# A state-space scan and windowed attention on one core: when a row is scaled, and how the inverse key sums reach the partitions that need them

## The chip, the cores and the metric

The kernel runs on one core of a Trainium2 chip. A core has TensorE (matrix products, "PE" in the profile, with its weight loads as "PEld"), VectorE ("DVE"), ScalarE ("ACT"), GpSimd ("POOL") and SyncE ("SP"), which here only issues transfers. Each engine works through its own list of instructions in order and waits at the head of the list until the inputs of the next instruction are there. The metric is device time in microseconds of one execution; lower is better.

## What is computed

The input `x` has 32 sequences of 256 tokens with 256 channels each. Two networks follow each other, and `x` is added to the result at the end. All is in 32-bit floating point. The first is a gated state-space layer; its core is a scan over the tokens:

```python
xr, gate = jnp.split(x @ W_in.T, 2, axis=-1)          # 512 channels each
xc = silu(causal_conv4(xr + t_emb[:, None, :]))
xn = layernorm(xc) * ln_g + ln_b
Bm, Cm, dt = jnp.split(xn @ W_xproj.T, 3, axis=-1)     # 16 states each
Ad = 1.0 + tanh(dt @ W_dt.T + b_dt) * 0.01 * -tanh(A_log)
Bd = Bm * minimum(norm(xn), 1.0)
def step(h, inputs):                                   # 256 steps, one after the other
    ad, bd, xt, ct = inputs
    h = jnp.clip(h * ad[:, :, None] + bd[:, :, None] * xt[:, None, :], -10.0, 10.0)
    return (h, jnp.einsum('bd,bdh->bh', ct, h))
y = (ys + D * xn) * silu(gate) @ W_out.T
```

The second is two layers of attention in windows of 128 tokens (each window sees itself and the one before), with 8 heads of 64, followed by a gated feed-forward part:

```python
q, k, v = heads(shift_token(x) @ wqkv)
q, k = rotary(l2norm(q) * qs, l2norm(k) * ksc)
attn = softmax(where(mask, -max, 8.0 * q @ k.T))
x = x + (attn @ v) @ wo
a, g = split(layernorm(shift_token(x)) @ w1 + b1)
x = x + (a * gelu(g)) @ w2 + b2
```

## The kernel before

**Groups and sequences.** The 32 sequences are worked in 4 groups of 8 (`GB`). The scan of a group holds the 8 sequences times 16 states on the 128 partitions and the 512 channels in the free dimension; it takes 256 steps, in 8 chunks of 32 (`CH`). Attention and feed-forward then take one sequence and one layer at a time: 4 groups x 2 layers x 8 sequences = 64 passes, called "sequences" below. While attention works on group g, the scan of group g + 1 runs beside it. The first scan group therefore has no attention beside it, and the last attention group no scan.

**A step of the scan.** The normalised tokens of a chunk are stored to device memory (`xnd`). For each token, `load_rows` (line 634) loads its 8 rows back, each repeated over 16 partitions, into a tile `xrep` of [128, 512] from the pool `xp`, which has 7 buffers. `scale_row` (line 654) multiplies it in place on ScalarE by a factor per partition, `beta`, which is computed once per chunk (lines 579 to 606). `step` (line 662) adds it to the state and clips, on VectorE, and frees the buffer. `read_out` (line 672) forms four steps' outputs on TensorE (`y`). In the first group, half of the rows come from a product on TensorE instead (`spread_rows`, line 639). The text asks for the load of token t at slot t - 6, for the scaling at t - 1 and for the step at t (lines 838 to 854).

**Attention of one sequence.** `scores` (line 1103) forms key-by-query products and their exponentials `pT` on ScalarE. `sums` (line 1131) adds them over the keys with a product by ones, so that the sum of head h stands on 16 partitions, and takes the reciprocal `rinv` on VectorE (line 1145): [128, 256], where the 8 heads lie at every 16th partition. `values` (line 1148) forms the unnormalised output `oT`, [128, 4, 256]: four pairs of heads, 64 partitions per head. `divide` (line 1166) must therefore bring the inverse sum of each head to the 64 partitions of its output. It does so with a product on TensorE by a table of ones and zeros, `head_rows` (filled in `head_table`, line 354), into PSUM tiles `rb`, and VectorE multiplies. `finish` calls `project_out` (line 958), whose product is `ps_wo`. `FeedForward` follows: `normalise`, `apply` and `spread` (layer norm, with a power on GpSimd), `widen` (product `pa`, then gelu to `ag` on ScalarE), `product`, and `narrow` (product `po_f`). The exponential and the gelu need different function tables on ScalarE, so a table load stands between them where they alternate.

**What sets the order.** The program text first lists the work by stages: 8 stages (`ST`) per sequence, and each part of sequence n gets a stage (lines 1332 to 1371); between stages, a proportional number of scan slots is put in. The compiler's scheduler then orders each engine's list from that text. It keeps dependences, and takes next what is ready first by its own model of durations, with the order of the text as priority. An instruction given to `keep_in_program_order` is issued after every instruction of its engine that stands before it in the text; for all others the scheduler may move them ahead. Transfers are issued by SP in the order that results, each after the events that it waits for; a load of `xrep` waits until the step that used the buffer before is done. All PSUM tiles share one pool of 8 banks.

Of the kernel before, what the change touches and what calls it, by code (L numbers as in the profile page):

```python
# [10 lines left out]
FP = mybir.dt.float32  # L11
# [8 lines left out]
P = 128  # L20
S = 256
# [15 lines left out]
HEADS = 8  # L37
DH = 64
# [35 lines left out]
def kernel(  # L74
# [29 lines left out]
    nc = tc.nc  # L104
# [4 lines left out]
    const = ctx.enter_context(tc.tile_pool(name="const", bufs=1))  # L109
# [35 lines left out]
    ident = const.tile([P, P], FP, tag="ident", name="ident")  # L145
# [17 lines left out]
    for j in range(NJ):  # L163
# [18 lines left out]
        out=mask_t[:, 0:W], in_=mask_t[:, 0:W], compare_op=ALU.is_ge, fill=MASKED_LOW,  # L182
# [3 lines left out]
        out=mask_t[:, W : 2 * W], in_=mask_t[:, W : 2 * W], compare_op=ALU.is_ge,  # L186
        fill=MASKED_LOW, base=0, pattern=[[-1, W]], channel_multiplier=1,
    )


    head_cols = const.tile([P, 2, 32], FP, tag="head_cols", name="head_cols")
    nc.gpsimd.memset(head_cols, 0.0)
    head_rows = const.tile([P, HEADS, DH], FP, tag="head_rows", name="head_rows")
    for r in range(2):
        nc.gpsimd.memset(head_cols[:, r, r * 16 : (r + 1) * 16], 1.0)
    rc_sb = const.tile([P, L, NW, 2, DH], FP, tag="rc_sb", name="rc_sb")
# [19 lines left out]
    for i in range(2):  # L216
        t = const.tile([P, NI * (P + GB)], FP, tag=f"ly{i}", name=f"ly{i}")
# [3 lines left out]
    def program(ctx, exact):  # L221
# [14 lines left out]
        def constants(at):  # L236
# [117 lines left out]
            def head_table(h):  # L354
                row = 32 * (h // 2) + 16 * (h % 2)
                tc.keep_in_program_order(
                    nc.gpsimd.tensor_copy(
                        head_rows[:, h, :], ident[:, row : row + 1].broadcast_to([P, DH])
                    )
                )  # L360

            at(-43, load_w)
            at(-34, fold_1)
            at(-32, fold_2)
# [20 lines left out]
        def group_scan(g):  # L385
# [14 lines left out]
            def at(s, what, *args):  # L400
                agendas[-1].setdefault(s, []).append(partial(what, *args))
# [252 lines left out]
            def scale_row(c, t):  # L654
                if by_tensor(t):
                    ck[c]["rep", t] = xp.tile([P, DI], FP, tag="xrep", name="xrep")
                bx = ck[c]["rep", t]
                nc.scalar.activation(  # L658
                    bx, ck[c].pop(("bx", t), bx), AF.Copy, scale=ck[c]["beta"][:, t : t + 1]
                )  # L660

            def step(c, t):
                bx = ck[c].pop(("rep", t))
# [174 lines left out]
            for c in range(NCH):  # L838
                s0 = c * CH
                at(s0 - 43, load_x, c)  # L840
                for ch in range(NC_):
                    at(s0 - 40 + 2 * ch, project, c, ch)
                for ch, s in enumerate((13, 16, 17, 18)):
                    at(s0 + s, project, c, NC_ + ch)
                at(s0 - 27, raw_sums, c)
                for j in range(NJ):
                    at(s0 - 26 + 4 * j, norm_turn, c, j)
                at(s0 - 8, figures_out, c)
                for t in range(CH):
# [227 lines left out]
        class Attention:  # L1077
# [70 lines left out]
            def values(self, b):  # L1148
# [14 lines left out]
                    nc.scalar.copy(oT[:, i0 : i0 + 2], ov)  # L1163
                self.o[b] = oT

            def divide(self, b):
                for i0 in range(0, HEADS // 2, 2):
                    rb = ps_w.tile([P, 2, S], FP, tag="w", name="rb")
                    for i in range(2):
                        h = 2 * (i0 + i)  # L1170
                        nc.tensor.matmul(
                            rb[:, i],
                            head_rows[:, h : h + 2].rearrange("p r d -> p (r d)"),
                            self.rinv,
                            start=True,
                            stop=True,
                        )
# [151 lines left out]
        def stage(n, i, what, *args):  # L1329
            stages.setdefault(ST * n + i, []).append(partial(what, *args))  # L1330

        def attend(n, at, b, nxt):

            stage(n, 0, at.turn, b, 1)
            stage(n, 3, at.scores, b, 0, 0, 2)
            stage(n, 2, at.scores, b, 1, 0, HEADS // 2)
            stage(n, 5, at.scores, b, 0, 2, 2)
            stage(n, 7, at.sums, b)
            stage(n, 7, at.values, b)
            stage(n + 1, 2, at.divide, b)  # L1340
            stage(n + 1, 5, at.finish, b)
            if nxt is not None:
                for w in range(NW):
                    for i, a in ((0, 2), (1, 0), (1, 1)):
                        stage(n, 3 * w + i, nxt[0].project, nxt[1], w, a)
                stage(n, 6, nxt[0].turn, nxt[1], 0)

        def feed(n, g, l, b):
            ff = FeedForward(g, l, b)
            for w in range(NW):  # L1350
                stage(n + 1, 7 + w, ff.normalise, w)
                stage(n + 2, 0 + w, ff.apply, w)
                stage(n + 2, 1 + w, ff.spread, w)
            for m in range(NM):
                stage(n + 2, 3 + m, ff.widen, m)
                stage(n + 2, 4 + m, ff.product, m)
            for d in range(KM):
                stage(n + 3, 2 + d, ff.narrow, d)

        def fetch(n, g, l, b):  # L1360

            if b == GB - 1 and (g, l) != (NG - 1, L - 1):
                nl = (l + 1) % L
                for i, a in ((5, 2), (6, 0), (6, 1)):
                    stage(n - 1, i, load_weights, nl, "qkv", a)
                stage(n + 1, 7, load_weights, nl, "wo")
                for m in range(NM):
                    stage(n + 2, 5 + m, load_weights, nl, "w1", m)
                stage(n + 3, 5, load_weights, nl, "w2")
            if l == L - 1 and g < NG - 1:  # L1370
                stage(n + 6, 2, load_res, g + 1, b)

# [159 lines left out]
```

## Time and profile before

The median of three runs is 3999.52 us (3998.8 to 4003.98). The profiled execution took 3989.48 us, and its span, from the first to the last instruction, is 3987.7 us at a mean granted TensorE clock of 0.983.

| Work | Line | Engine | Count | One |
|---|---|---|---|---|
| product `rb` (recorded as two passes per instruction) | 1171 | PE | 512 | 379 ns |
| multiplication `oT` by `rb`, 128x512 | 1179 | DVE | 128 | 676 ns |
| reciprocal `rinv`, 128x256 | 1145 | DVE | 64 | 1748 ns |
| scaling of a loaded row | 658 | ACT | 896 | 722 ns |
| step of the scan | 665 | DVE | 1024 | 807 ns |
| table loads before exponentials and gelus | 1127, 1255 | ACT | 185 and 186 | 1283 ns |
| loads of rows, 256 KB each | 637 | SP | 896 | 515 ns to issue |

Times are those of the profile's groups and tiles (medians where it gives them). A group's busy time counts overlapping instructions once. "Idle before" a group is the time that its engine stood still just before, and the name after the arrow is what ended it. The stretches, the waits and the timeline are views of the same recording; a sequence of the attention is repeated at a fixed distance in time in the last stretch, so that one can be read for all.

The lines that follow are the first groups of the costliest, with their idle time and releaser at the end:

```profile
L658 ACT ACTIVATE xrep<-xrep,beta 128x512 f32<-128x512 f32 x896 | 631.1, 722 | 692.2 <-DMA xrep<-xnd 532.4
L665 DVE CUSTOM_DVE_ANT_0 h<-h,xrep,lim 128x512 f32<-128x512 f32 x1024 | 918.6, 897 | 52.7 <-PE y L677 12.5
L912 PE MATMUL ps_qkv<-qkv,res 128*128 128x512 f32 x1536 | 718.0, 604 | 34.6 <-ACT qT L956 21.7
```

### The profile page before, as it was taken

The numbers are of one execution on the slowest core, as the hardware profiler recorded it, in microseconds if no ns is written. First come the engines' busy times: TensorE is split into PE (matmuls) and PEld (weight loads), VectorE is DVE, ScalarE is ACT, GpSimd is POOL, SyncE is SP. The second block draws the span as 40 slices with busy tenths as digits, with TensorE's granted clock in tenths as the row PEclk, the third lists the DMA queues.
The fourth block names the chain that finished last, engine by engine and source line by source line (L and its number), as shares of the span: only waits on it lengthen the run. The fifth ranks groups of instructions, "written<-read, shape, count | busy, mean of one in ns | idle before, by whom it ended". The sixth has DMA issues, their size and how long they took to land.

```text
span 3987.7 us, 57891 instructions
## 1 busy us (share of the span) xinstructions
PE 3769.4 (95%) x20540; PEld 2359.2 (59%) x20540; DVE 2638.7 (66%) x5241; ACT 2321.3 (58%) x3893; POOL 1739.2 (44%) x1784
## 2 busy tenths in 40 slices
PE   7899889999999999999999999999999999999999
PEld 3333345666656666666666666566666666666666
DVE  6888887777766766767676677676677544444443
ACT  3555556666666566566666656556666555555553
POOL 4443364444444444544445444344444343433431
PEclk8999899999999999999999999999999999999999
DMA  5444533333433434233343434323333111000000
GB/s 152 116 119 118 159 111 110 89 107 103 106 98 97 124 109 128 84 93 94 91 112 94 118 106 116 101 83 101 94 101 103 36 36 44 1 17 20 18 14 23
DMA packets 360414, 353.51 MB, mean 89 GB/s; under 512 B 173795, under 2 KB 220212, under 8 KB 359988
## 3 DMA queue, kind: packets, MB, share of 16 engines
q1 hardware_dynamic: 275666, 337.71, 29.4%
q10 hardware_dynamic: 84450, 12.01, 1.9%
q8 instruction: 165, 2.70, 0.3%
q14 instruction: 133, 1.09, 0.1%
HBM read 314.49 MB, written 33.55 MB: 87 GB/s over the span
## 4 chain that ended last, share of the span: by engine, by line
PE 44%; DVE 16%; ACT 13%; DMA 11%; POOL 9%; issue 5%; ACTq 1%; SPq 0%; DVEq 0%; POOLq 0%
DMA xrep<-xnd 10%; PE ps_qkv L912 9%; PE pa L1247 8%; PE po_f L1275 5%; DVE h L665 5%; PE y L677 3%; ACT xrep L658 3%; PE ps_wo L962 3%; PE sc L1118 3%; PE ov L1156 2%; POOL rn L944 2%; ACT L1255 2%; DVE acc L454 2%; PE ps_in L407 2%; ACT L1127 2%
## 5 line engine op out<-in xcount | busy, mean ns | idle before, releaser
L658 ACT ACTIVATE xrep<-xrep,beta 128x512 f32<-128x512 f32 x896 | 631.1, 722 | 692.2 <-DMA xrep<-xnd 532.4
L665 DVE CUSTOM_DVE_ANT_0 h<-h,xrep,lim 128x512 f32<-128x512 f32 x1024 | 918.6, 897 | 52.7 <-PE y L677 12.5
L912 PE MATMUL ps_qkv<-qkv,res 128*128 128x512 f32 x1536 | 718.0, 604 | 34.6 <-ACT qT L956 21.7
L1247 PE MATMUL pa<-hT,w 128*128 128x256 f32 (+1 forms) x3072 | 693.0, 388 | 28.0 <-ACT pT L1127 26.8
L936 POOL TENSOR_TENSOR rot<-rot,swp 128x512 f32<-128x512 f32 x256 | 344.1, 1344 | 766.3 <-DVE swp L933 621.5
L1247 PEld LDWEIGHTS pa<-hT,w 128*128 128x128 f32 (+1 forms) x3072 | 502.4, 179 | 192.1 <-issue 63.3
L1263 DVE SCALAR_TENSOR_TENSOR ag<-pa,b_sb,ag 128x256 f32<-128x256 f32 (+1 forms) x448 | 213.1, 476 | 594.6 <-ACT ag L1255 593.2
L912 PEld LDWEIGHTS ps_qkv<-qkv,res 128*128 128x128 f32 x1536 | 279.2, 192 | 314.6 <-issue 247.4
L944 POOL TENSOR_TENSOR rn<-ss,neg_half 128x8 f32<-128x8 f32 x256 | 444.2, 1735 | 11.5 <-DVE ss L942 1.6
L1275 PE MATMUL po_f<-ag,w 128*128 128x256 f32 (+1 forms) x1536 | 385.4, 392 | 17.9 <-DVE res L1286 9.3
L677 PE MATMUL y<-h,ly 128*32 128x512 f32 x2048 | 369.1, 620 | 20.1 <-DVE h L665 19.5
L1275 PEld LDWEIGHTS po_f<-ag,w 128*128 128x128 f32 (+1 forms) x1536 | 273.9, 189 | 124.3 <-issue 44.4
L407 PE MATMUL ps_in<-xg,w_in_sb 128*128 128x256 f32 x1024 | 285.9, 410 | 18.0 <-DMA xg<-in_xT_dram 10.4
L945 POOL TENSOR_TENSOR rot<-rot,rn 128x512 f32<-128x512 f32 x256 | 287.7, 1124 | 20.0
L1206 POOL TENSOR_TENSOR rstd<-ve,neg_half 128x1 f32<-128x1 f32 x128 | 77.0, 602 | 486.6 <-DVE ve L1204 486.6
L407 PEld LDWEIGHTS ps_in<-xg,w_in_sb 128*128 128x128 f32 x1024 | 190.8, 199 | 145.7 <-issue 62.0
L928 DVE TENSOR_TENSOR rot<-ps_qkv,rc_sb 128x512 f32<-128x512 f32 x256 | 175.6, 686 | 139.0 <-ACT sq L925 137.8
L1127 ACT ACTIVATE pT<-sc 128x512 f32<-128x512 f32 x384 | 208.3, 594 | 94.9 <-PE sc L1118 93.3
L454 DVE SCALAR_TENSOR_TENSOR acc<-xr,wc_sb,acc 128x256 f32<-128x256 f32 x384 | 203.4, 532 | 89.2 <-POOL acc L443 88.1
L1127 ACT ACT_TABLE_LOAD x185 | 237.4, 1283 | 24.5 <-PE sc L1118 21.5
L1255 ACT ACTIVATE ag<-pa,b_sb 128x256 f32<-128x256 f32 x320 | 151.7, 474 | 156.8 <-PE pa L1247 152.4
L1255 ACT ACT_TABLE_LOAD x186 | 238.6, 1283 | 3.3
(149 smaller groups left out, 5765.7 us busy)
## 6 DMA issues: line engine op xcount, KB each, us to landing
xrep<-xnd SPq DMA_DIRECT2D x896, 256.0 KB
xnd<-xn SPq DMA_DIRECT2D x64, 256.0 KB
qkv<-in_wqkv_dram SPq DMA_DIRECT2D x24, 512.0 KB
xd<-xnd SPq DMA_DIRECT2D x192, 64.0 KB
w<-in_w_dram SPq DMA_DIRECT2D x80, 128.0 KB
xg<-in_xT_dram SPq DMA_DIRECT2D x64, 128.0 KB
ys<-yo ACTq DMA_DIRECT2D x64, 128.0 KB
res<-ys SPq DMA_DIRECT2D x32, 256.0 KB
```

Of the source, the lines that this page charges most:

```text
L407: nc.tensor.matmul(ps, w_in_sb[:, k, ch * P : (ch + 1) * P], ck[c]["xg"][:, k], start=(k == 0), stop=(k == KM - 1),)
L658: nc.scalar.activation(bx, ck[c].pop(("bx", t), bx), AF.Copy, scale=ck[c]["beta"][:, t : t + 1])
L665: nc.vector._custom_dve(TENSOR_ADD_SAT, out=h_new, in0=state["h"], in1=bx, s0=ck[c]["lim"][:, 0, t : t + 1], s1=ck[c]["lim"][:, 1, t : t + 1],
L677: nc.tensor.matmul(ck[c]["y", hb][32 * q : 32 * q + 32, :], ly[hb % 2][:, 32 * t : 32 * t + 32], ck[c].pop(("h", hb * TB + t)), start=(i = ...
L912: nc.tensor.matmul(ps, res[b][:, k, t0 : t0 + W], wt["qkv", a][:, k], start=(k == 0), stop=(k == KM - 1),)
L936: nc.gpsimd.tensor_add(rot, rot, swp)
L944: nc.gpsimd.tensor_tensor(rn, ss, neg_half, ALU.pow)
L945: nc.gpsimd.tensor_mul(rot, rot, bc(rn, 2, DH))
L1127: nc.scalar.activation(p, banks[r], AF.Exp)
L1247: nc.tensor.matmul(pg if x else pa, wt["w1", m][:, k, x], self.h[:, k], start=(k == 0), stop=(k == KM - 1),)
L1255: nc.scalar.activation(ag[0:n], pg, AF.Gelu, bias=b1g)
L1275: nc.tensor.matmul(self.po[:, d], wt["w2", 0][r0 : r0 + n, m, d * P : (d + 1) * P], self.ag[m][r0 : r0 + n], start=(m == 0), stop=(m == le ...
```

## The change

There are three edits, and what follows from them.

1. *Scaling.* From the second group on, each scaling is given to `keep_in_program_order`, and all scalings are asked for one slot earlier (t - 2 instead of t - 1).
2. *Inverse sums.* The product by `head_rows` and the table itself go. `put_inverse` stores the 8 rows of `rinv` (8 KB) to a tile `inv` in device memory; `load_inverse` reads it back twice, for the even and for the odd heads, each row repeated over 64 partitions, into `rb`, [128, 4, 256], now in SBUF (one buffer). `divide` becomes one multiplication. The tile takes space in SBUF, and `xp` has 6 buffers instead of 7.
3. *Stages.* Store, load, multiplication and output product get the stages 0, 2, 4 and 6 of the next sequence's time (the multiplication was at 2, the output product at 5), and the feed-forward and the weight loads that belong to it come one stage later.

```diff
-    head_rows = const.tile([P, HEADS, DH], FP, tag="head_rows", name="head_rows")
...
-        xp = ctx.enter_context(tc.tile_pool(name="xp", bufs=7, reuse_waits="tile"))
+        xp = ctx.enter_context(tc.tile_pool(name="xp", bufs=6, reuse_waits="tile"))
...
-            for h in range(HEADS):
-                at(100 + 2 * h, head_table, h)
...
-                nc.scalar.activation(
+                scaled = nc.scalar.activation(
                     bx, ck[c].pop(("bx", t), bx), AF.Copy, scale=ck[c]["beta"][:, t : t + 1]
                 )
+                if not alone:
+
+                    tc.keep_in_program_order(scaled)
...
-                    at(s0 + t - 1, scale_row, c, t)
+                    at(s0 + t - 2, scale_row, c, t)
...
+            def put_inverse(self):
+                self.inv = dp.tile([HEADS, S], FP, tag="inv", name="inv")
+                nc.sync.dma_start(out=self.inv, in_=self.rinv[0 : P : P // HEADS])
+
+            def load_inverse(self):
+
+                rb = ap_.tile([P, HEADS // 2, S], FP, tag="rb", name="rb", bufs=1)
+                inv = self.inv.rearrange("(i r) t -> r i t", r=2)
+                for r in range(2):
+                    nc.sync.dma_start(out=rb[r * DH : (r + 1) * DH], in_=bc(inv[r], 0, DH))
+                self.rb = rb
+
             def divide(self, b):
-                for i0 in range(0, HEADS // 2, 2):
-                    rb = ps_w.tile([P, 2, S], FP, tag="w", name="rb")
-                    for i in range(2):
-                        h = 2 * (i0 + i)
-                        nc.tensor.matmul(
-                            rb[:, i],
-                            head_rows[:, h : h + 2].rearrange("p r d -> p (r d)"),
-                            self.rinv,
-                            start=True,
-                            stop=True,
-                        )
-                    o = self.o[b][:, i0 : i0 + 2]
-                    nc.vector.tensor_mul(o, o, rb)
+                nc.vector.tensor_mul(self.o[b], self.o[b], self.rb)
...
-            stage(n + 1, 2, at.divide, b)
-            stage(n + 1, 5, at.finish, b)
+            stage(n + 1, 0, at.put_inverse)
+            stage(n + 1, 2, at.load_inverse)
+            stage(n + 1, 4, at.divide, b)
+            stage(n + 1, 6, at.finish, b)
...
-                stage(n + 1, 7 + w, ff.normalise, w)
-                stage(n + 2, 0 + w, ff.apply, w)
-                stage(n + 2, 1 + w, ff.spread, w)
+                stage(n + 1, 8 + w, ff.normalise, w)
+                stage(n + 2, 1 + w, ff.apply, w)
+                stage(n + 2, 2 + w, ff.spread, w)
             for m in range(NM):
-                stage(n + 2, 3 + m, ff.widen, m)
-                stage(n + 2, 4 + m, ff.product, m)
+                stage(n + 2, 4 + m, ff.widen, m)
+                stage(n + 2, 5 + m, ff.product, m)
             for d in range(KM):
-                stage(n + 3, 2 + d, ff.narrow, d)
+                stage(n + 3, 3 + d, ff.narrow, d)
```

Each engine's list is ordered anew by the scheduler for the changed text, so instructions that no edit names can stand elsewhere than before.

More of the change, by code (lines that the diff above doesn't have):

```diff
@@ L352, in tables @@
                 )
[L354 to L358, printed above, removed]
-                    )
-                )
             at(-43, load_w)
@@ L1164, in values @@
                 self.o[b] = oT
-            def divide(self, b):
-                for i0 in range(0, HEADS // 2, 2):
-                    rb = ps_w.tile([P, 2, S], FP, tag="w", name="rb")
-                    for i in range(2):
-                        h = 2 * (i0 + i)
-                        nc.tensor.matmul(
-                            rb[:, i],
-                            head_rows[:, h : h + 2].rearrange("p r d -> p (r d)"),
-                            self.rinv,
-                            start=True,
-                            stop=True,
-                        )
-                    o = self.o[b][:, i0 : i0 + 2]
-                    nc.vector.tensor_mul(o, o, rb)
+            def put_inverse(self):
[7 more added lines that the diff above has]
+                self.rb = rb
+            def divide(self, b):
+                nc.vector.tensor_mul(self.o[b], self.o[b], self.rb)
             def finish(self, b):
@@ L1365, in fetch @@
                     stage(n - 1, i, load_weights, nl, "qkv", a)
-                stage(n + 1, 7, load_weights, nl, "wo")
+                stage(n + 2, 0, load_weights, nl, "wo")
                 for m in range(NM):
-                    stage(n + 2, 5 + m, load_weights, nl, "w1", m)
-                stage(n + 3, 5, load_weights, nl, "w2")
+                    stage(n + 2, 6 + m, load_weights, nl, "w1", m)
+                stage(n + 3, 6, load_weights, nl, "w2")
             if l == L - 1 and g < NG - 1:
```

## The prediction

> **What bounds the kernel now.** I read the page's engine shares first, then the busy time by stretch, then the waits, and last single stretches of the timeline.
>
> ```profile
> PE 3769.4 (95%) x20540; PEld 2359.2 (59%) x20540; DVE 2638.7 (66%) x5241; ACT 2321.3 (58%) x3893; POOL 1739.2 (44%) x1784
> ```
>
> TensorE is busy in 95% of the span, VectorE (DVE) in 66%. The stretches say where the missing 5% lies. Columns: stretch, its length, busy microseconds (and instructions) of PE, weight load, DVE, ACT and POOL, granted clock, DMA share, GB/s.
>
> ```profile
> 0.00:487.00 487.00, 415.00 (x1552) 170.10 (x1552) 410.62 (x769) 264.08 (x489) 198.57 (x289) 0.93 0.47 129
> 487.00:600.00 113.00, 102.41 (x516) 53.40 (x516) 90.14 (x162) 59.87 (x108) 70.10 (x62) 0.91 0.44 127
> 600.00:3100.00 2500.00, 2373.68 (x13434) 1529.42 (x13435) 1756.72 (x3486) 1559.24 (x2618) 1137.75 (x1148) 0.99 0.37 103
> 3130.00:3900.00 770.00, 770.00 (x4412) 527.82 (x4406) 332.59 (x732) 393.73 (x606) 314.39 (x267) 1.00 0.08 22
> 3900.00:3988.00 88.00, 78.36 (x442) 59.66 (x438) 27.00 (x59) 27.91 (x49) 7.80 (x9) 0.98 0.06 20
> ```
>
> There are three regimes: the first scan group alone (to 487), scan and attention side by side (to 3100), and attention alone (to the end). In the last, TensorE never stops: 770.00 of 770. In the middle it is idle for 2500 - 2373.7 = 126.3 us, and for 10.6 more in 487 to 600. So work taken off TensorE is gained nearly in full there, and 137 us of stalls are the second thing to win.
>
> The product that the change removes, by the same stretches (PE, weight load, DVE only), and one run of it at the end:
>
> ```profile
> 600.00:3100.00 2500.00, 81.51 (x344) 61.92 (x344) 55.38 (x86) 0.99 0.37 103
> 3130.00:3900.00 770.00, 34.06 (x144) 25.96 (x144) 24.75 (x36) 1.00 0.08 22
> ```
>
> ```profile
> 3937.37 1.89 PE L1171 MATMUL rb<-rinv,head_rows 128*128 128x256 f32 x8
> 3939.10 2.95 PE L1275 MATMUL po_f<-ag,w 128*128 128x256 f32 x12
> ```
>
> It is 8 passes for each of 64 sequences (344/8 = 43 in the middle, 18 in the third, 1 before, 2 after). A run shows 1.89 us busy, but the next product starts 1.73 us after it began; the rest is pipeline overlap. 1.73 us is its price.
>
> Who stalls TensorE, in 600 to 3100 (who waits for whom: total, times, longest):
>
> ```profile
> ACT xrep L658 <- DMA xrep<-xnd: 429.3, 258, 7.7
> ACT xrep L658 <- DVE beta L606: 112.1, 20, 6.6
> PE pa L1247 <- ACT pT L1127: 26.8, 15, 1.9
> PE ps_qkv L912 <- ACT qT L956: 21.7, 14, 2.2
> PE ov L1156 <- DVE ag L1263: 13.6, 12, 2.1
> ```
>
> ScalarE (ACT) stands 541 us at the head of its queue before a scaling whose input is not there, and TensorE in turn waits for what is queued behind. One case in full:
>
> ```profile
> 1836.87 0.72 ACT L658 ACTIVATE xrep<-xrep,beta 128x512 f32<-128x512 f32 x1 [6.63 <-DVE beta L606]
> ...
> 1837.92 1.28 ACT L1127 ACT_TABLE_LOAD   x1
> ...
> 1839.21 1.09 ACT L1127 ACTIVATE pT<-sc 128x512 f32<-128x512 f32 x2
> ...
> 1839.86 1.99 PE L1247 MATMUL pa<-hT,w 128*128 128x256 f32 x8 [1.93 <-ACT pT L1127]
> ```
>
> The scaling holds ACT 6.63 us, then a table load of 1.28, then the exponential; TensorE loses 1.93 us until that frees a bank.
>
> [...] in the last stretch there is no gap and passes follow each other at 1.73/8 = 0.216 us: for removed work, occupancy decides. [...] above the activation starts 1.29 us after the load starts[...] Here a store to device memory holds the load that depends on it for up to 4.2 us (129.09 to 133.26):
>
> ```profile
> 129.09 0.34 SPq L545 DMA_DIRECT2D xnd<-xn  x1
> 129.65 0.52 SPq L637 DMA_DIRECT2D xrep<-xnd  x1
> 133.26 1.35 SPq L694 DMA_DIRECT2D xq<-xnd  x2
> ```
>
> **The change part by part**, against the profiled execution: 3989.5 us, 1.8 of it outside the span of 3987.7.
>
> *The product goes.* 64 x 1.73 = 110.7 us off TensorE: 76 of it up to 3100, 31 between 3130 and 3900, 3.5 after. No other TensorE work is added. Value -110.7.
>
> *Two multiplications become one.* DVE did 2 x 0.69 us per sequence from PSUM; now one of 1024 columns from SBUF. No such row exists; doubling 0.69 gives at most 1.4[...]. DVE is idle 30% and more of each stretch; counted 0.
>
> *The round trip.* SP gets three transfers per sequence, 192 in all: a store of 8 KB and two broadcasts of 256 KB, the size of an xrep load. The 512 KB per sequence are 33 MB more beside 353; in the middle about 9 GB/s beside 103. The store waits for the reciprocal and holds SP till then; the first broadcast waits for the store's landing ([...] the 4.2 above), issues take about 0.5 each, and a load lands about 3.6 us after its issue (in the trace xrep issues at 1672.71 and its held scaling starts at 1676.33). In the changed program's order one or two xrep loads stand between the two broadcasts. From the reciprocal's end to landed: [...] 7 to 11 us. Behind the store on SP stand xrep loads; a row is consumed every 2500/702 = 3.6 us and six buffers give about 14 us from issue to scaling two rows ahead, so 5 us of hold are covered. The multiplication is what waits: in the changed DVE order it stands 9 instructions behind the reciprocal in the attention-only stretch, and alternately 37 and 10 in the middle. After 10 instructions DVE has followed TensorE through ov, a wide product and tp_h, some 10 us after rs by the rows above and below. So the wait is 0 to 2 us in half of the sequences. Queued behind it on DVE are normalisation statistics, tp_hn and the rotations, which TensorE wants some 5 us later. I take +5 in all, ends 0 and +60.
>
> *Scaling in program order, one slot earlier in the text.* It removes nothing; it puts each scaling behind the ACT work traced before it, instead of straight behind its load. The 541 us of held ACT should go; what then comes last is PSUM release by ACT and DVE at their real speed.
>
> *Stages moved by one.* The multiplication, the output product and the feed-forward come one or two stages later. In the built order this lowers the table loads from 6 to 4 per sequence (124 in all): 124 x 1.283 = 159 us off ACT, in front of just those exponentials and gelus that TensorE waits for.
>
> Of the 137 us of stalls, the named waits on ACT add to about 70 and those on DVE's ag, itself held by ACT, to 17. I take 60 off, not all 87, since the new order brings waits of its own. Ends: +20 (they take more than they give) and -130.
>
> *Six xrep buffers, not seven; no head_rows.* In the first group a row takes 387/249 = 1.55 us, and half the rows come by DMA; issue to landing, scaling and step are 3.6 + 0.7 + 0.8 = 5.1 us against 5 x 1.55 = 7.8 available. Counted 0, ends 0 and +15. Eight copies of 0.7 us leave POOL, beside DVE work: 0.
>
> *The end.* For the last sequence the product ran at 3937.37 and ps_wo at 3947.26; reciprocal end 3931.9 plus 7 to 11 plus 1.4 is 3940 to 3944, so ps_wo hides it. 0.
>
> Sum: 3989.5 - 110.7 - 60 + 5 = 3823.8 us. The median of the runs, 3999.5, is 10 us above the profiled one; added, 3834 us.
>
> **Rivals.** (a) *The stalls stay.* Step waits for scaling with two rows of lead instead of five, or DVE for the broadcast, and TensorE is idle as before. For it: the order is planned, not measured, and DVE had 1757 of 2500 us busy. Against: ACT has the most held time. 3989.5 - 110.7 + 10 = 3889. (b) *All stalls go.* The last stretch shows TensorE can run without one. Against: DVE had half the load there. 3989.5 - 110.7 - 137 + 10 = 3752. (c) *Slower: the multiplication waits for the round trip.* If the broadcast lands so late that TensorE loses more than the 1.73 us per sequence it saved, the change loses; at 3 us per sequence, 64 x 3 - 110.7 = +81, so 4081. It decides from a round trip of some 14 us on. For it: 9 or 10 instructions are little cover. Against: 7 to 11 us by the rows, and TensorE wants nothing of it for 5 us more. (d) *No change*, gain and wait cancelling by chance.
>
> **Numbers.** Forecast as in the sum (3780 to 3885) 0.66; (a) 0.18; (b) 0.08; (c) 0.06; (d) 0.02. About 0.2%, 8 us, is what a measurement can tell from no change. Faster 0.66 + 0.18 + 0.08 = 0.92, same 0.02, slower 0.06. The range takes in part of (a) and most of (b): 3765 to 3905.
>
> **What would show it.** No rb matmul on PE, and a period near 41.2 us for a sequence in the last stretch, where ps_qkv to ps_qkv is 42.97 now; about 124 fewer table loads; ACT's wait for xrep loads well under 100 us; PE idle in the middle near 75 us, not 126. It is wrong if DVE waits long for rb, if step waits for ACT in the middle, or if the last stretch shows gaps on PE.

## The result and the profile after

The changed kernel takes 3859.53 us (median of 4 runs, 3857.8 to 3861.79) against 4001.75 us (3998.8 to 4004.76) for the kernel before on the same chip: 0.9642 of it, interval 0.963 to 0.9654, or 142 us less. The profiled execution took 3861.79 us, its span is 3860.0 us, 127.7 less than before, at the same mean clock of 0.983.

First the engine shares of the changed kernel, as the page shows them, to compare with the page's line of the kernel before.

```profile
PE 3671.3 (95%) x20028; PEld 2261.0 (59%) x20028; DVE 2629.5 (68%) x5177; ACT 2163.9 (56%) x3769; POOL 1754.4 (45%) x1776
```

TensorE has 512 records fewer and is busy 98.1 us less, and ACT 157 us less; TensorE's share is still 95%, because the span fell with it. Now the busy time by stretch (columns as before: stretch, length, busy and instructions of PE, weight load, DVE, ACT and POOL, clock, DMA share, GB/s).

```profile
487.00:600.00 113.00, 104.06 (x533) 53.93 (x532) 92.81 (x169) 60.03 (x111) 74.00 (x68) 0.94 0.50 132
600.00:3000.00 2400.00, 2293.06 (x13067) 1465.08 (x13066) 1752.01 (x3433) 1449.77 (x2528) 1149.89 (x1142) 0.99 0.45 116
3100.00:3800.00 700.00, 699.58 (x4059) 470.38 (x4061) 304.28 (x662) 332.08 (x539) 281.28 (x240) 1.00 0.13 33
```

The last stretch is as full as before, so the missing product is a gain there. In the middle TensorE is idle for 2400 - 2293.1 = 106.9 us; the kernel before had 125.3 in the same stretch. Most of the stalls are still there, but the places that waited have changed. The waits of the changed kernel in 600 to 3000 (engine and line, what it waited for: total, times, longest; in order of total, lines of other places left out):

```profile
DVE ag L1254 <- ACT ag L1246: 102.5, 60, 4.0
...
DVE h L656 <- ACT xrep L646: 89.1, 81, 3.4
DVE oT L1170 <- DMA rb<-inv: 82.8, 21, 5.8
...
ACT xrep L646 <- DMA xrep<-xnd: 37.8, 29, 2.3
...
PE ov L1147 <- DVE ag L1254: 21.9, 14, 2.6
...
PE ps_qkv L903 <- DVE ag L1254: 18.2, 13, 1.4
...
PE po_f L1266 <- DVE res L1277: 16.6, 10, 2.3
...
PE po_f L1266 <- DVE fo L1277: 10.8, 8, 2.3
```

ACT's wait for loads of rows, 429.3 us in 600 to 3100 before, is down to 37.8. In its place DVE waits twice: 89.1 us before steps for ACT's scalings, and 82.8 us, in 21 places, for the broadcast `rb`. TensorE, which waited for ACT (`pT`, `qT`), now waits for DVE (`ag`, `res`, `fo`). One of the 21 places, from the timeline of the changed kernel (start, duration, engine and line, operation; in brackets the idle time before it and what ended it):

```profile
2636.91 1.75 DVE L1136 RECIPROCAL rinv<-rs 128x256 f32<-128x256 f32 x1
2638.69 0.61 SPq L1159 DMA_DIRECT2D inv<-rinv  x1
2640.42 0.61 SPq L1166 DMA_DIRECT2D rb<-inv  x1
...
2642.39 0.59 SPq L1166 DMA_DIRECT2D rb<-inv  x1
...
2649.06 1.22 DVE L1170 TENSOR_TENSOR oT<-oT,rb 128x1024 f32<-128x1024 f32 x1 [4.08 <-DMA rb<-inv]
...
2651.21 0.48 DVE L1254 SCALAR_TENSOR_TENSOR ag<-pa,b_sb,ag 42x256 f32<-42x256 f32 x1
...
2664.75 3.50 PE L1266 MATMUL po_f<-ag,w 128*128 128x256 f32 x9 [1.91 <-DVE res L1277]
```

The round trip, from the reciprocal's end at 2638.66 to the multiplication, is 10.4 us. DVE has nothing left to do in front of it and stands still for 4.08 us. Behind it in DVE's list stand the product `ag` and the residual `res`, and some 15 us later TensorE stands 1.91 us for that `res`. That one place doesn't prove the link: just before `res` DVE also stood 1.85 us for a result of GpSimd (`stat`, line 542). What these readings can't say is which of the waits costs time, and which part of the change brought the gain. The experiments are about that.

### The profile page after: what moved, and what is told of

The parts are those of the page before. It is cut to its first block, busy times and chain, and to the rows that moved or that the text cites. A ratio compares the mean times of both kernels' runs of the same rounds, so it can differ in the third digit from the quotient of the medians.

```text
span 3860.0 us, 57026 instructions
## 1 busy us (share of the span) xinstructions
PE 3671.3 (95%) x20028; PEld 2261.0 (59%) x20028; DVE 2629.5 (68%) x5177; ACT 2163.9 (56%) x3769; POOL 1754.4 (45%) x1776
## 4 chain that ended last, share of the span: by engine, by line
PE 48%; DVE 20%; POOL 13%; DMA 8%; ACT 6%; issue 4%; SPq 1%; ACTq 0%; POOLq 0%; DVEq 0%
PE ps_qkv L903 9%; PE pa L1238 9%; PE po_f L1266 6%; DVE h L656 6%; POOL rn L935 5%; PE y L668 4%; DMA rb<-inv 3%; DVE acc L442 3%; PE ps_wo L953 3%; PE ov L1147 3%; PE sc L1109 3%; ACT xrep L646 2%; POOL rot L936 2%; DVE rot L919 2%; PE ps_in L395 2%
## 5 line engine op out<-in xcount | busy, mean ns | idle before, releaser
L656 DVE CUSTOM_DVE_ANT_0 h<-h,xrep,lim 128x512 f32<-128x512 f32 x1024 | 941.7, 920 | 133.8 <-ACT xrep L646 96.8
L646 ACT ACTIVATE xrep<-xrep,beta 128x512 f32<-128x512 f32 x896 | 622.7, 718 | 139.3 <-DMA xrep<-xnd 99.1
L1238 PE MATMUL pa<-hT,w 128*128 128x256 f32 (+1 forms) x3072 | 684.5, 385 | 1.0 <-DVE zT L737 1.0
L935 POOL TENSOR_TENSOR rn<-ss,neg_half 128x8 f32<-128x8 f32 x256 | 453.4, 1771 | 28.0 <-DVE ss L933 17.5
L1266 PE MATMUL po_f<-ag,w 128*128 128x256 f32 (+1 forms) x1536 | 397.8, 401 | 40.0 <-DVE res L1277 16.6
L668 PE MATMUL y<-h,ly 128*32 128x512 f32 x2048 | 381.1, 618 | 11.6 <-DVE h L656 10.9
L916 ACT ACTIVATE sq<-ps_qkv 128x512 f32<-128x512 f32 x256 | 151.5, 596 | 238.9 <-PE ps_qkv L903 195.2
L442 DVE SCALAR_TENSOR_TENSOR acc<-xr,wc_sb,acc 128x256 f32<-128x256 f32 x384 | 187.8, 491 | 94.0 <-POOL acc L431 92.0
L953 PE MATMUL ps_wo<-oT,wo 128*128 128x256 f32 x1024 | 231.7, 379 | 0.0
```

Source lines behind the costliest of these rows:

```text
L442: nc.vector.scalar_tensor_tensor(acc, xr[:, :, k : k + CH], wc_sb[:, ch, k : k + 1], acc, ALU.mult, ALU.add,)
L646: scaled = nc.scalar.activation(bx, ck[c].pop(("bx", t), bx), AF.Copy, scale=ck[c]["beta"][:, t : t + 1])
L656: nc.vector._custom_dve(TENSOR_ADD_SAT, out=h_new, in0=state["h"], in1=bx, s0=ck[c]["lim"][:, 0, t : t + 1], s1=ck[c]["lim"][:, 1, t : t + 1],
L668: nc.tensor.matmul(ck[c]["y", hb][32 * q : 32 * q + 32, :], ly[hb % 2][:, 32 * t : 32 * t + 32], ck[c].pop(("h", hb * TB + t)), start=(i = ...
L935: nc.gpsimd.tensor_tensor(rn, ss, neg_half, ALU.pow)
L953: nc.tensor.matmul(po[:, d], wt["wo", 0][:, c, d * P : (d + 1) * P], oT[:, c, :], start=(c == 0), stop=(c == NC_ - 1),)
```

## The experiments

Kernels that ran together share the runs of the kernel before on their chip; its medians were 4000.26 us beside runs 1 to 4, 3989.36 beside 5 to 8, 3998.54 beside 9 to 11 and 3980.11 beside 12. So kernels that ran together are compared by their times, others by the ratio to before, where 0.001 is 4 us. "Last step" is when the last step of the scan starts in the profiled execution, "rest" what follows it to the end of the span, and "idle" TensorE's idle time in 600 to 3000.

| Kernel | Ratio (interval) | Median us | Last step | Rest | Idle |
|---|---|---|---|---|---|
| before | 1 | | 3116.4 | 871.3 | 125.3 |
| changed | 0.9642 (0.963 to 0.9654) | 3859.53 | 3019.1 | 840.9 | 106.9 |
| 1 scaling undone | 1.0029 (1.0021 to 1.0037) | 4012.53 | 3153.5 | 847.9 | 201.5 |
| 2 scaling alone | 0.9656 (0.9643 to 0.967) | 3865.98 | 3000.0 | 865.0 | 28.0 |
| 3 stages alone | 1.0006 (0.9996 to 1.0017) | 4003.88 | 3115.0 | 885.2 | 120.2 |
| 4 product kept | 0.9713 (0.97 to 0.9726) | 3886.22 | 3009.1 | 875.3 | 39.1 |
| 5 product kept, six buffers | 0.9716 (0.9699 to 0.9733) | 3879.01 | 3005.1 | 875.1 | 40.6 |
| 6 no transfers | 0.9517 (0.9499 to 0.9536) | 3799.15 | 2959.6 | 840.3 | 57.7 |
| 7 transfers unread | 0.9529 (0.951 to 0.9547) | 3804.57 | 2963.5 | 840.3 | 65.8 |
| 8 transfers in the last 20 only | 0.9595 (0.9577 to 0.9612) | 3830.3 | 2995.4 | 832.8 | 28.5 |
| 9 multiplication held | 0.951 (0.9489 to 0.9532) | 3799.47 | 2957.1 | 840.6 | 59.3 |
| 10 held, old stages | 0.9496 (0.9475 to 0.9516) | 3795.4 | 2960.9 | 830.8 | 52.5 |
| 11 scaling undone, multiplication held | 0.9988 (0.9979 to 0.9996) | 3995.84 | 3142.1 | 848.6 | 196.2 |
| 12 scaling held, at t - 1 | 0.9724 (0.9708 to 0.974) | 3873.39 | 3009.2 | 864.2 | 29.8 |

### 1 to 4: the parts one by one

My first theory, called M in the texts, was that the scaling edit had freed TensorE and that the wait for the broadcast had taken that back. Its rival S was that the scaling edit was worth nothing. Both took the 110.7 us of the product for granted.

*Run 1* is the changed kernel with this edit:

```diff
-                if not alone:
-
-                    tc.keep_in_program_order(scaled)
...
-                    at(s0 + t - 2, scale_row, c, t)
+                    at(s0 + t - 1, scale_row, c, t)
```

> The changed kernel with the scaling as it was before: left to the scheduler and asked for at t - 1. Theory M (the scaling edit freed TensorE, and the multiplication's wait for its broadcast took the gain back): ACT stands long before scalings again, 300 us or more for loads of rows, TensorE loses some 30 us more, and the time is near 3890. Theory S (the scaling edit is worth nothing: what ACT no longer waits, DVE waits before its steps): 3860, within 8 us of the changed kernel, with DVE's wait of 89 us for ACT's xrep mostly gone.

Measured: 4012.53 us, slower than the kernel before. Both theories missed by over 100 us. ACT waits again, as M said, and TensorE stands idle for 201.5 us, 76 more than before the change. Part of the time is TensorE's clock: its mean granted clock over the span is 0.976 here and 0.983 in the changed kernel. By the spans that is (1 - 0.976) x 4001 = 96 us of full speed lost against (1 - 0.983) x 3860 = 66, an estimate from the means (in the profile before, the four passes of `ps_qkv` in 1070.4 to 1073.6, at a granted clock of 0.50, took 787 to 1221 ns, the median pass of 600 to 3000 took 592); whether the lower clock is a cause or an effect of the gaps, no run here tests. Two lines of its waits in 600 to 3000:

```profile
ACT xrep L646 <- DMA xrep<-xnd: 481.2, 276, 7.6
...
DVE oT L1167 <- DMA rb<-inv: 33.5, 18, 3.7
```

*Run 2* is the kernel before with the scaling edit alone:

```diff
+                if not alone:
+
+                    tc.keep_in_program_order(scaled)
...
-                    at(s0 + t - 1, scale_row, c, t)
+                    at(s0 + t - 2, scale_row, c, t)
```

> The kernel before with the scaling edit alone (program order, t - 2); product by head_rows, stages and seven buffers as before. Theory M: it is worth 30 to 40 us without a broadcast to wait for, 3960 to 3970. Theory S: 4000, with ACT's 430 us before loads of rows replaced by waits of DVE before its steps.

Measured: 3865.98 us. With every product still on TensorE, this one edit gives 134 us, where M gave it 30 to 40 and S nothing; by the ratios the whole change gives only 6 us more, and their intervals overlap. The middle stretch of this run, and its waits there:

```profile
600.00:3000.00 2400.00, 2371.98 (x13585) 1536.34 (x13585) 1796.32 (x3509) 1573.08 (x2639) 1132.41 (x1156) 1.00 0.39 107
```

```profile
DVE h L668 <- ACT xrep L658: 141.2, 60, 4.5
...
DVE ag L1266 <- ACT ag L1258: 82.2, 65, 5.8
...
PE ov L1159 <- DVE ag L1266: 7.7, 14, 0.6
```

TensorE is idle for 28.0 of 2400 us, and its largest wait is 7.7. Yet DVE waits 141.2 us before steps for scalings, half as much again as in the changed kernel. So that wait, which looks as bad on the page as the one for the broadcast, does TensorE little harm. One thing more: TensorE's busy time in the whole span is 3747.6 us here and 3769.4 before, for the same 20540 records. So about 22 us of the busy time before were not work. Most of it is the clock, by an estimate from the mean clocks: (1 - 0.983) x 3987.7 = 68 us of full speed lost before, (1 - 0.986) x 3865 = 54 here. Where the rest comes from isn't shown.

*Run 3* is the kernel before with the stages of the change:

```diff
-            stage(n + 1, 2, at.divide, b)
-            stage(n + 1, 5, at.finish, b)
+            stage(n + 1, 4, at.divide, b)
+            stage(n + 1, 6, at.finish, b)
...
-                stage(n + 1, 7 + w, ff.normalise, w)
+                stage(n + 1, 8 + w, ff.normalise, w)
...
-                stage(n + 3, 2 + d, ff.narrow, d)
+                stage(n + 3, 3 + d, ff.narrow, d)
```

> The kernel before with the stages of multiplication, output product and feed-forward moved as in the change, and nothing else. 124 table loads fewer, 159 us less on ACT. Theory M: ACT frees banks sooner, TensorE gains 20 to 30 us, 3970 to 3980. Theory S: ACT was not what ended last, 4000 within 8 us. In the stretch of attention alone TensorE has no gap, so both expect no change there.

Measured: 4003.88 us, ratio 1.0006 with 1 in its interval. A table load is gone 124 times, and nothing is gained, as S said. In the last stretch there is even a loss that nobody expected: from one reciprocal to the next (ten periods in the timeline) it is 43.30 us, where the kernel before has 42.97.

*Run 4* has run 2's and run 3's edits together, on the kernel before, with its product and seven buffers.

> The kernel before with the scaling edit and the moved stages together, the product on TensorE kept. It differs from the changed kernel in the product against the round trip alone (and the seventh buffer). Theory M: the stalls do go when no broadcast is waited for, TensorE idle in the middle near 60 us, 3935 to 3945, so that the transfers in place of the product are worth only some 80 of their 110.7. Theory S: the stalls stay without the broadcast too, 3970 to 3985, and the transfers are worth 110 to 125.

Measured: 3886.22 us, TensorE idle for 39.1 us in the middle. The stalls do go without a broadcast, and more of them than M said: the time is some 50 us below M's range. The step from here to the changed kernel is worth only 0.9713 - 0.9642 = 0.0071, some 28 us, where 110.7 us of TensorE work go. The traces say where: the rest after the last step falls by 34.4 us, and the last step itself comes 10.0 us later although 76 us of work went before it. Some 86 us of new stalls have come in there. (The next expectation counts from the end of the first group, which also came 7.6 us earlier in the changed kernel, and so has 18 and 94.)

### 5 to 8: what the transfers cost beside the scan

*Run 5* is run 4 with `xp` at six buffers.

```diff
-        xp = ctx.enter_context(tc.tile_pool(name="xp", bufs=7, reuse_waits="tile"))
+        xp = ctx.enter_context(tc.tile_pool(name="xp", bufs=6, reuse_waits="tile"))
```

> The kernel with scaling edit and moved stages and the product kept (3886), with six xrep buffers in place of seven. The question: from that kernel to the changed one TensorE loses 76 us of work beside the scan, and yet the stretch up to the last step of the scan grows by 18 us, so some 94 us of new stalls came with the transfers. Theory X (it is the buffer): 3960 to 3980. Theories W (DVE's wait at the multiplication), Q (the transfers hold SyncE's queue and with it the loads of rows) and Z (a bound other than TensorE): within 8 us of 3886.

Measured: ratio 0.9716 against 0.9713. The seventh buffer is worth nothing here, and X falls.

*Run 6* leaves the round trip and the division out of the changed kernel:

```diff
-            stage(n + 1, 0, at.put_inverse)
-            stage(n + 1, 2, at.load_inverse)
...
-                nc.vector.tensor_mul(self.o[b], self.o[b], self.rb)
+                o = self.o[b].rearrange("p (a i) t -> p a (i t)", a=2)
+                nc.vector.tensor_mul(o, o, bc(dskip_sb, 1, 2))
```

> The changed kernel without the division by the key sums: the store and both broadcasts are left out, and the multiplication (same size, same engine) takes a table that is in SBUF from the start. So the output's attention is not normalised. Theories W and Q: all 94 us of stalls go, 3765 to 3780. Theory X and theory Z: 3850 to 3860, TensorE still idle for some 100 us or more in the middle.

*Run 7* has the same multiplication, but issues store and broadcasts.

> As the run without transfers, but store and broadcasts are issued as in the change; only the multiplication takes the table from SBUF and not their result (the division is left out of the computation). Theory W (the wait at the multiplication costs it all): as without transfers, 3765 to 3785. Theory Q (what costs is that SyncE's queue is held and loads of rows come late): 3850 to 3865, as changed, and 80 us slower than without transfers. Theories X and Z: 3850 to 3860, both alike.

Measured: 3799.15 us without transfers, 3804.57 with transfers that nobody reads. Both are some 20 us above the ranges that fitted W, and 45 and more below those of X and Z. The 33 MB of traffic and SP's 192 issues cost some 5 us, and the two intervals overlap, so Q falls. From unread to read is 0.9642 - 0.9529 = 0.0113, some 45 us by the ratios and 55 by the medians, and in the traces the last step moves from 2963.5 to 3019.1, 55.6 us. That is about what the multiplication's wait costs, for the 82.8 us that the waits show. Z isn't ruled out in full: even without transfers TensorE idles for 57.7 us in the middle.

One caution: in these two runs the multiplication also moved forward in DVE's list. Beside the scan it stands only 1 or 2 instructions behind the reciprocal in most sequences, and DVE waits in front of it for ACT's `oT` (14.7 us in 600 to 3000 in run 7). So the step from run 7 to the changed kernel is not the wait for `rb` alone. Run 9 has no such doubt.

*Run 8* is run 2 with the transfers in place of the product for the last 20 sequences only, where no scan runs.

```diff
-            stage(n + 1, 2, at.divide, b)
+            if n >= 44:
+                stage(n + 1, 0, at.put_inverse)
+                stage(n + 1, 1, at.load_inverse)
+                stage(n + 1, 3, at.divide_loaded, b)
+            else:
+                stage(n + 1, 2, at.divide, b)
```

`divide_loaded` multiplies twice by halves of `rb` that lie in two `xrep` buffers.

> The kernel before with the scaling edit (3866), seven buffers, original stages; the product on TensorE is kept for sequences 0 to 43, and the transfers take its place in the last 20, where no scan runs beside them (into two xrep buffers each, which are free by then; two multiplications). All theories: 20 x 1.73 = 35 us less, 3831, if a period there is 41.2 us; 3866 or more if the multiplication, 7 instructions behind the reciprocal, makes DVE and then TensorE wait.

Measured: 3830.3 us; the rest after the last step is 832.8, 32.2 less than in run 2. The period there is 41.24 us in the median, 42.97 less the 1.73 of the product: in this stretch, where TensorE has no gap, the removed work is gained one for one. (By the ratios to run 2, on two chips, the gain is 24 us, by the medians 36.)

### 9 to 12: the wait taken away, and the scaling again

In the changed kernel's list the multiplication stands 37 and 10 DVE instructions behind the reciprocal by turns, from the 15th to the 42nd sequence. The trace shows which ones wait: those with 37 start some 19 us behind the reciprocal's end and never wait, and those with 10 start 9.8 to 12.4 us behind it, when the broadcast lands. These are 14 of the 21 places; the other 7 lie in the first 14 sequences, where the distance varies.

*Run 9* holds it back and changes nothing else in the changed kernel:

```diff
-                nc.vector.tensor_mul(self.o[b], self.o[b], self.rb)
+                tc.keep_in_program_order(
+                    nc.vector.tensor_mul(self.o[b], self.o[b], self.rb)
+                )
```

> The changed kernel with one edit: the multiplication too is held in program order, so that it stands 41 to 47 DVE instructions behind the reciprocal beside the scan (24 after it) and not 37 and 10 by turns (9 after it). Nothing is left out, all transfers are read. Theory W (DVE's wait at the multiplication is what was lost): DVE waits for the broadcast no more, and the time comes near that of the run with unread transfers, 3800 to 3815. Against it: what stands later on DVE delays the output product, and the gain is lost again, 3840 to 3860.

Measured: 3799.47 us, 0.951 (0.9489 to 0.9532); 60 us less than the changed kernel by the medians, 53 by the ratios. The same work in this run's timeline, at another time:

```profile
2586.30 1.75 DVE L1136 RECIPROCAL rinv<-rs 128x256 f32<-128x256 f32 x1
2588.08 0.61 SPq L1159 DMA_DIRECT2D inv<-rinv  x1
2589.82 0.61 SPq L1166 DMA_DIRECT2D rb<-inv  x1
2591.78 0.59 SPq L1166 DMA_DIRECT2D rb<-inv  x1
2615.64 1.22 DVE L1171 TENSOR_TENSOR oT<-oT,rb 128x1024 f32<-128x1024 f32 x1
```

and its middle stretch and waits there:

```profile
600.00:3000.00 2400.00, 2340.67 (x13452) 1501.75 (x13452) 1805.15 (x3501) 1483.02 (x2580) 1202.27 (x1167) 1.00 0.45 117
```

```profile
DVE h L656 <- ACT xrep L646: 121.9, 118, 3.4
...
DVE ag L1256 <- ACT ag L1248: 49.1, 60, 4.2
...
PE ps_qkv L903 <- DVE ag L1256: 18.2, 13, 1.4
...
PE ov L1147 <- DVE ag L1256: 17.6, 11, 3.0
```

The multiplication starts 27.6 us behind the reciprocal, and the view has no wait for `rb` left at all. TensorE's waits of `po_f` for `res` and `fo` are gone from the top, and its idle time falls from 106.9 to 59.3 us. The wait before steps is larger than in the changed kernel (121.9 against 89.1), and the kernel is faster: again it is not the one that counts. Theory W stands. Part of the price may be the clock, whose mean in the middle is 1.00 here and 0.99 in the changed kernel; no run isolates it.

*Run 10* also takes the feed-forward's stages back.

```diff
-            stage(n + 1, 2, at.load_inverse)
-            stage(n + 1, 4, at.divide, b)
-            stage(n + 1, 6, at.finish, b)
+            stage(n + 1, 1, at.load_inverse)
+            stage(n + 1, 3, at.divide, b)
+            stage(n + 1, 5, at.finish, b)
...
-                stage(n + 3, 3 + d, ff.narrow, d)
+                stage(n + 3, 2 + d, ff.narrow, d)
```

> As the run with the multiplication held late, but with the feed-forward and the weight loads at the stages that the kernel before had; store, broadcasts, multiplication and output product at stages 0, 1, 3 and 5. The multiplication stands 35 to 38 DVE instructions behind the reciprocal beside the scan, 19 after it; six table loads per sequence as before. With the product kept, the old stages were 10 us better in the last stretch (period 42.97 against 43.30) and 6 before it. So 3785 to 3795 if this holds without the product too; 3805 to 3825 if the shorter cover makes DVE wait.

Measured: 3795.4 us. The rest after the last step is 830.8, 9.8 less than in run 9, as expected; the last step comes 3.8 later. The gain over run 9, 4 us, is within the intervals. It is the fastest kernel of the study beside run 9, and both beat the changed one. Here the waits of `po_f` for `res` and `fo` are back (20.3 and 16.0 us, more than in the changed kernel), with no wait for `rb`. So those two waits of TensorE are not by themselves the mark of the late broadcast.

*Run 11* asks why the transfers gained nothing in run 1. It is run 1 with run 9's edit.

> The changed kernel with the scaling as before (left to the scheduler, t - 1; it was 4012) and the multiplication held in program order, 44 to 46 instructions behind the reciprocal beside the scan. It asks why the transfers gained nothing where the scaling was not held in order. If it was the wait at the multiplication there too (33.5 us in the middle): 3900 to 3930. If held scalings on ACT set the pace beside the scan, so that TensorE's 76 us of work there were not on the path: the stretch up to the last step stays at 2660 us or more and only the last 20 sequences gain, 3965 to 3985.

Measured: 3995.84 us, and the last step at 3142.1. No wait for `rb` is left, and yet ACT waits 491.1 us for loads of rows, and TensorE idles for 196.2 us. So with scalings left to the scheduler the stretch beside the scan has a pace that taking the product out doesn't quicken: TensorE's idle time is 71 us above that of the kernel before, for 76 us of work taken out. Only the last sequences gain. (The time is 11 us above the range that fitted this.)

*Run 12* parts the scaling edit in two: held in order, but at t - 1.

```diff
-                    at(s0 + t - 2, scale_row, c, t)
+                    at(s0 + t - 1, scale_row, c, t)
```

> The kernel before with scalings held in program order, but asked for at t - 1 as before, not at t - 2 (that was 3866); everything else as before. If the order on ACT is what brought the gain: 3860 to 3890, with ACT hardly waiting for loads of rows. If the earlier slot was needed (DVE otherwise stands before its steps until ACT has scaled, and TensorE behind DVE): 3920 or more, with DVE's wait for xrep well over the 141 us of the t - 2 run.

Measured: 3873.39 us, a ratio of 0.9724 against 0.9656 for run 2. By the ratios the order is worth 110 us and the slot 27; by the medians and by the profiled spans the slot is worth 7 and 8. The two ran on different chips, so the size of the slot's share is open. The order is most of it.

## Why the prediction was right, and where not

The time forecast was 3834 us with a range of 3765 to 3905; the kernel took 3859.53. The direction and most of the size were right, but through terms that were wrong by more than the difference: that the sum came out within 26 us is luck, since the scaling's gain was set too low and the product's gain and the wait's price were wrong the other way. The terms, with the profiled executions put in a chain of edits (before, run 2, 4, 5, 6, 7, changed), so that they add up to the -127.7 of the spans:

| Term | Forecast | Last step | Rest | Sum |
|---|---|---|---|---|
| scaling in order and earlier | -60, with the next | -116.4 | -6.3 | -122.7 |
| stages moved | within the -60 | +9.1 | +10.3 | +19.4 |
| six buffers | 0 | -4.0 | -0.2 | -4.2 |
| product goes | -110.7 | -45.5 | -34.8 | -80.3 |
| transfers issued | 0 | +3.9 | 0 | +3.9 |
| multiplication waits | +5 | +55.6 | +0.6 | +56.2 |

A single profile differs from another by some us, and the one before lay 12 below the median of 4001.75, so the first term is rather 134. Runs 6 and 7 also have the multiplication at another place. With run 9 in their stead, the product with its transfers gives -48.0 and -34.5, and the wait costs 62.0 and 0.3.

- *"The 541 us of held ACT should go": right.* ACT's wait for loads in the middle is 37.8 us, and the edit did the most of all.
- *"I take 60 off, not all 87": mis-sized.* The term is 123 to 134 us for the scaling alone. I added up the waits of TensorE that named ACT (70) and `ag` (17), but a wait is charged to whoever came last. In run 2 idle time fell by 97 us, and 22 us more had been in what counts as busy, so waits that named neither must have hung on the held ACT too; they were not followed one by one.
- *"124 x 1.283 = 159 us off ACT, in front of just those exponentials and gelus that TensorE waits for": failed.* The 124 table loads did go (ACT lost 157 us), but run 3 shows no gain, and run 4 is 20 us slower than run 2. What was held up was ACT behind its scalings, not ACT by its amount of work.
- *"The product goes. Value -110.7": right in the last stretch only.* There 20 x 1.73 = 34.6 was forecast and 34.8 measured. Beside the scan 45.5 to 48.0 of 76 came, and with scalings left to the scheduler (runs 1 and 11) nothing. "Gained in full" held only where TensorE had no gaps.
- *"I take +5 in all": the step that failed most, at 56 us.* The round trip itself was right, 10.4 us in the place shown (9.8 to 12.4 in those like it) for 7 to 11 forecast, and so were its place and the half of the sequences. Its first part is the landing of the store: the prediction shows one of 4.2 us in the profile before; the shorter one, on which its lower end of 7 rests, it doesn't show. The changed kernel's trace has 1.73 us from the issue of the store to that of the broadcast that waits for it (2638.69 to 2640.42 above), and a median of 1.75 over the 64 sequences. Of the wait I said 0 to 2 us; it was 82.8 us in 21 places, a mean of 3.9. And I counted on TensorE wanting what is queued behind it only 5 us later, so that little of a wait would reach it. Run 9 shows that 64% (by the ratios) to 75% (by the spans) of the time that DVE stood still reached the end.
- *Rival (c), "slower: the multiplication waits for the round trip", deciding from some 14 us on:* the mechanism is the one at work, but its price, about 1.3 us per sequence beside the scan (55.6 / 43), stayed below what the product gave. A round trip of 10.4 us, not 14, was enough for it. *Rival (a)* gave 3889, about as far off as my own sum, and its first reason, that step waits for scaling, is there with 89.1 us; runs 2 and 9 show it to cost little.
- *The signs.* Of the signs that the prediction was wrong, two came: DVE waits long for `rb` (82.8 us), and step waits for ACT in the middle (89.1 us). TensorE is idle there for 106.9 us, not near 75. The missing table loads and the shorter wait of ACT came as said.
- *Nothing for the multiplication and the buffers: right.* The new multiplication takes 1.22 us (1218 ns in the mean of 64) instead of two of 0.68 (679 ns in the mean of 128). The eight copies into `head_rows` that GpSimd no longer makes took 230 to 700 ns each. ("Idle 30% and more of each stretch" was misread: DVE is busy for 84% and 80% of the first two stretches, 410.6 of 487 and 90.1 of 113 us. Nearly all of the multiplications come later.)
- *"A period near 41.2 us":* it is 41.57, that is 43.30 of the moved stages less 1.73. I had not thought that moved stages cost anything in a stretch where TensorE never stops. Two reciprocals that follow each other in the last stretch, in the changed kernel's timeline:

```profile
3187.41 1.76 DVE L1136 RECIPROCAL rinv<-rs 128x256 f32<-128x256 f32 x1 [0.48 <-PE rs L1128]
...
3228.98 1.76 DVE L1136 RECIPROCAL rinv<-rs 128x256 f32<-128x256 f32 x1 [0.48 <-PE rs L1128]
```

The reason why scalings set the pace when left to the scheduler is read from the traces, not isolated by a run. From the issue of a row's load to its scaling it was 4.8 us (median over groups 2 to 4) and from scaling to step 17.8; in run 2 it is 16.8 and 3.7. The buffers before held rows that were already scaled, each load was issued late, and ACT stood at the head of its list until it landed. Holding the order turned this round.

What stays open: why moved stages cost 0.33 us per sequence in the last stretch. From start to start of its passes in the traces, `pa` takes 0.23 us more there and `ps_qkv` and `ov` 0.09 each, `tp_h` 0.09 less, at a clock of 1.00 in both; the reason isn't shown. Open too is what makes TensorE idle for 50 to 60 us in the middle of runs 6, 9 and 10, where 28 remain with the product. The waits that the view names are for DVE's `ag` in run 9 (43.3 us) and for `res` and `fo` in run 10 (36.3); what stands behind them was not followed.

## What to carry over

Add up what a wait holds behind it, not only the waits of the engine you want to fill: here 141 us of DVE standing before steps left TensorE idle for only 28 us, while 83 us before one multiplication cost 53 to 62. The product moved into transfers paid more where the consumer stood later than the round trip of 9.8 to 12.4 us: 27.6 us behind the reciprocal in the place shown of run 9, which took 3799.47 us against 3859.53. Check the place of such a consumer in its engine's list, in every phase of the kernel, and hold it there if the scheduler puts it earlier. Here removed work counted in full only in the stretch in which its engine had no gap (34.8 us for 34.6 forecast, but 45.5 to 48.0 of 76 beside the scan), so price each stretch by itself.

## What the runs showed that was not expected

- Transfers of 520 KB per sequence on a queue that also feeds the scan cost some 5 us over 64 sequences (run 7 against run 6; the intervals overlap), with the middle's traffic up from 107 to some 117 GB/s.
- Taking work off TensorE can leave the time as it was, or make it longer: run 1 against run 3, ratio 1.0029 against 1.0006, with 110 us of work less (and with the round trip and a buffer less). Without the wait for the round trip it was 0.9988 (run 11), still far from 110 us.
- A buffer less in the pool of rows made no difference (run 5 against run 4, 0.9716 against 0.9713).
